# Unread whole-array products in the attention steps with heads of 8

## The chip, the cores and the metric

The kernel runs on one core of one Trainium2 chip. The metric is the device time of an execution in microseconds; lower is better. A core has a matrix engine (TensorE, in the profile PE for products and PEld for weight loads), a vector engine (VectorE, DVE), an activation engine (ScalarE, ACT), GpSimd (POOL) and DMA queues (SPq and others). [...]

## The reference

A batch of 16 sequences of 256 tokens with 128 channels goes through four layers. Each layer adds an attention (16 heads) and a feed-forward network. All four attentions look at the same context of 1601 rows of 64 channels; layers 0 and 2 also have an attention of the sequence to itself. In layers 0, 1 and 3 a head has 8 channels, in layer 2 it has 32. Cut to what matters:

```python
# layers 0, 1 and 3: x (16, 256, 128), ctx (16, 1601, 64), H = 16, D = 8
q = heads(norm(x) @ Wq); k = heads(ctx @ Wk); v = heads(ctx @ Wv)
a = softmax(einsum('bhqd,bhkd->bhqk', q, k) * D ** -0.5)
x = x + merge(einsum('bhqk,bhkd->bhqd', a, v)) @ Wo
x = x + ffn(norm(x))
# layer 2: the same with D = 32
```

## The kernel before, in words

**Two sequences at a time.** The kernel takes the sequences in eight rounds of two lanes. The list `seq` has, for every round, layer 0 of both, then layer 1 of both, then 2, then 3. Each entry is one attention over the context, and this main line of attentions is the frame of the whole program.

**Slabs and steps.** An attention is cut into four slabs of four heads (`Slab`). Four heads stand at partitions 0, 32, 64 and 96, so that a score product uses 32 rows of the array. With heads of 8 the 32 rows hold the high and low parts of queries and keys, which gives the float32 product from a shorter format. The 1601 keys are 13 tiles of 128 rows; a slab has seven steps of two tiles each, and the seventh has one tile of 65 keys.

**What a step does on TensorE, in program order.** The loop at the end of `model` writes the instructions in the order in which they are to run (`tc.manual_schedule()`), and TensorE takes its products in that order:

1. About half of the step's maxima of the *next* slab: a product of queries by 400 keys into a bank (`maxima`, from line 544), which VectorE reduces to a row maximum (line 552). A slab has 32 of them, five or six to a step.
2. The step's scores, transposed, into a double bank `st` (`st_ops`), with the maxima subtracted by bfloat16 products of ones by `nmT`. ScalarE turns them into probabilities (`exps`, line 464).
3. The rest of the step's maxima.
4. The weighing of the step before (`weigh_back`, which calls `weigh`): probabilities times values into the slab's accumulator bank `av`. With heads of 8, each of four heads has 9 columns (8 values and a sum) and only the first half of the bank, `av[:, 0, :]`, is used; with heads of 32 the second half takes the sums.
5. Two slots (`slot()`; three ahead of layer 2). A slot lets each of the side programs go on to its next `yield`: feed-forward networks, norms, the attention of a sequence to itself, keys and values of coming attentions (`key_line`, `value_line`).

All products are issued through the helper `mm` at line 172, so the profile gives them one line, and they are told apart by tiles: `bank<-k,q` are maxima, `st<-q,k` and `st<-nmT,ones` scores, `bank<-p,v` the weighing. A weighing product in float32 has two rows in the trace.

**Banks.** `bank()` deals out four banks. One is held by `av`, so the maxima wait for VectorE after three. The slots' products take theirs from the same four.

**The end of a slab.** After the last weighing, `finish` copies `av[:, 0, :]` out with ScalarE, transposes and divides. The maxima of the next slab are gathered (`thirds`, on VectorE and GpSimd) and transposed (`shift`, TensorE), which makes its `nmT`.

**Constants.** `ident16` is a 128x128 identity and `ones16` a 128x128 block of ones, both bfloat16, made once at the start. The causal mask of the self-attentions uses `ident16` against a mask `caus` in the same way, with 512 columns.

Of the kernel before, what the change touches and what calls it, by code (L numbers as in the profile page):

```python
# [20 lines left out]
P = 128  # L21
# [53 lines left out]
def model(ctx: ExitStack, tc: tile.TileContext, d, out):  # L75
# [34 lines left out]
    ident16 = const.tile([P, P], BF16, name="ident16")  # L110
    nc.vector.tensor_copy(ident16, ident)
    ones16 = const.tile([P, P], BF16, name="ones16")
# [58 lines left out]
    def mm(o, l, r, start=True, stop=True, free=False):  # L171
        nc.tensor.matmul(out=o, lhsT=l, rhs=r, start=start, stop=stop, skip_group_check=free)  # L172
# [289 lines left out]
    def exps(att, sc, n, r):  # L462
        e = probs()
        nc.scalar.activation(e[:r, :, :n, :], sc[:r, :, :n, :], AF.Exp, scale=att.scale)  # L464
        return e

    def zeroed(att):
        a = bank().rearrange("p (u q) -> p u q", u=2)
        n = 1 if att.d8 else 2
        mm(a[:, :n, :], zero16[:, :P], zero16.unsqueeze(1).broadcast_to([1, n, T]), True, False, True)  # L470
        return a

    def weigh(att, s, av, pr, t0, n, r, last, heads=range(4), sums=True, values=True):
        for i in range(n):
            fin = last and i == n - 1
            if values:
                for g in heads:
                    m = 9 if att.d8 else 32
                    mm(av[32 * g : 32 * g + m, 0, :], att.value(s, t0 + i, g, r), pr[g // 2][:r, g % 2, i, :],
                       False, fin, True)  # L480
            if sums and not att.d8:
                for g in heads:
                    mm(av[32 * g : 32 * g + 32, 1, :], ones[:r, :32], pr[g // 2][:r, g % 2, i, :], False, fin, True)

    def normalised(att, s, av):
        if att.d8:
            y = chan("y8")[:, :T]
            evac(y, av[:, 0, :])
            yield
            t = bank()  # L490
            for q in range(2):
                nc.tensor.transpose(t[:, q * P : (q + 1) * P], y[:, q * P : (q + 1) * P], ident)  # L492
            tv = t[:, :T].rearrange("p (q g e) -> p q g e", q=2, g=4)
            rc = sm.tile([P, 2, 4], F32, tag="rc8", name=name("rc8"))
            nc.vector.reciprocal(rc, tv[:, :, :, 8])
            nc.vector.tensor_tensor(
                att.o[:, :, 32 * s : 32 * s + 32].rearrange("p q (g e) -> p q g e", g=4),
                tv[:, :, :, :8], rc.unsqueeze(3).broadcast_to([P, 2, 4, 8]), ALU.mult,
            )
        else:  # L500
            rc = chan("rc")[:, :T]
            nc.vector.reciprocal(rc, av[:, 1, :])  # L502
            nc.vector.tensor_tensor(att.o[:, s, :], av[:, 0, :], rc, ALU.mult)
# [23 lines left out]
    class Slab:  # L527
# [16 lines left out]
        def maxima(self):  # L544

            g, q, c, k0, k1 = self.todo.popleft()
            att, s = self.att, self.s
            p = bank()
            h = slice(32 * g, 32 * g + 32)

            def reduce():
                nc.vector.tensor_reduce(self.mx[:, q, g, c : c + 1], p[:, : k1 - k0], AX.X, ALU.max)  # L552

            return lambda: mm(p[:, : k1 - k0], att.q[h, s, q * P : (q + 1) * P], att.k[s][h, k0:k1]), reduce
# [501 lines left out]
    def advance(g):  # L1056
        try:
            return True, next(g)
        except StopIteration:
            return False, None  # L1060

    def begin():

        while began[0] < nb:
            b = began[0]
            n = None if b < LANES else seq.index((b - LANES, "l3"))
            if n is not None and not (n in k_done and n in v_done):
                return
            chains.append([None, load_ctx(b)])
            chains.append([b, life(b)])  # L1070
            began[0] += 1

    def slot():
        begin()
        if later:
            g = later.popleft()
            if advance(g)[0]:
                later.appendleft(g)
        for i, l in enumerate(lines):
            if i == turn[0] % 2:  # L1080
                advance(l)
        turn[0] += 1
        for c in list(chains):
            if c[0] is not None and c[0] in ready:
                if not ready[c[0]].done:
                    continue
                del ready[c[0]]
            alive, att = advance(c[1])
            if att is not None:
                ready[c[0]] = att  # L1090
            if not alive:
                chains.remove(c)

    def until(cond):
        for _ in range(2000):
            if cond():
                return
            slot()
        raise RuntimeError("the slots do not come to an end")
# [3 lines left out]
    def slab(i):  # L1103

        n, s = divmod(i, 4)
        if n >= len(seq):
            return None
        b = seq[n][0]
        until(lambda: b in ready and not ready[b].done and n in k_of and s in k_of[n])
        att = ready[b]  # L1110
        att.k, att.v = k_of[n], v_of.setdefault(n, {})
        slabs_of[i] = Slab(att, s, i % 2)
        return slabs_of[i]

    def finish(sl, i):

        yield from normalised(sl.att, sl.s, sl.av)
        if sl.s == 3:
            sl.att.done = True
        if not sl.att.d8 or sl.s == 3:  # L1120
            vp_room.give()

    with tc.manual_schedule():
        sl = slab(0)
        while sl.todo:
            for o in sl.maxima():
                o()
        sl.thirds()
        sl.shift()
        back = None  # L1130

        def weigh_back():

            nonlocal back
            if back is None:
                return
            sl, i, j, pr = back
            n = i // 4
            t0, m, r = sl.steps[j]
            if j == 0:  # L1140
                until(lambda: (0 if sl.att.d8 else sl.s) in v_of.get(n, {}))
                sl.att.v = v_of[n]
                sl.av = zeroed(sl.att)
            last = j == len(sl.steps) - 1
            weigh(sl.att, sl.s, sl.av, pr, t0, m, r, last)
            back = None
            if last:
                g = finish(sl, i)
                if advance(g)[0]:
                    later.append(g)  # L1150

        for i in range(4 * len(seq)):
            nxt = slab(i + 1)
            steps = sl.steps
            emitted = 0

            def maxima(want):

                nonlocal emitted
                ops = []  # L1160
                while nxt is not None and emitted < want:
                    a, c = nxt.maxima()
                    a()
                    ops.append(c)
                    emitted += 1
                for c in ops:
                    c()

            for j, (t0, m, r) in enumerate(steps):

                part = 32 * (j + 1) // (len(steps) - 1)
                if j < len(steps) - 1:
                    maxima(part - 3)
                elif nxt is not None:
                    nxt.thirds()
                sc = st_ops(sl.att, sl.s, t0, m, r, sl.nmT)
                pr = [exps(sl.att, t, m, r) for t in sc]
                if j < len(steps) - 1:
                    maxima(part)
                weigh_back()  # L1180
                back = (sl, i, j, pr)
                if j == len(steps) - 1 and nxt is not None:
                    nxt.shift()
                slot()
                slot()

                if i // 4 + 1 < len(seq) and seq[i // 4 + 1][1] == "l2":
                    slot()
            kp_room.give()
            sl = nxt  # L1190
        weigh_back()
        until(lambda: not chains and not later)

# [118 lines left out]
```

## Time and profile before

| | |
|---|---|
| time, median of 3 | 11,063.08 us (11,060.85 to 11,069.93) |
| the profiled execution's time | 11,069.08 us |
| its span, first to last instruction | 11,067.1 us |
| mean granted TensorE clock | 0.815 |
| instructions | 204,917 |
| PE products, and their busy time | 86,834, 9,761.1 us |
| VectorE, ScalarE, GpSimd busy | 5,929.3, 4,978.5, 952.3 us |

The table is from the profile's page. Busy time is the time in which an engine has an instruction under way; products overlap in the array, so a busy PE is not PE at its peak. "Granted clock" is the share of TensorE's clock that the chip let through. An arrow in a row such as `bank<-p,v` reads "written from". The chain of waits is the series of instructions that ended last, followed back from the end, at each step to what released it.

### The profile page before, as it was taken

The numbers are of one execution on the slowest core, as the hardware profiler recorded it, in microseconds if no ns is written. First come the engines' busy times: TensorE is split into PE (matmuls) and PEld (weight loads), VectorE is DVE, ScalarE is ACT, GpSimd is POOL, SyncE is SP. The second block draws the span as 40 slices with busy tenths as digits, with TensorE's granted clock in tenths as the row PEclk, the third lists the DMA queues.
The fourth block names the chain that finished last, engine by engine and source line by source line (L and its number), as shares of the span: only waits on it lengthen the run. The fifth ranks groups of instructions, "written<-read, shape, count | busy, mean of one in ns | idle before, by whom it ended". The sixth has DMA issues, their size and how long they took to land.

```text
span 11067.1 us, 204917 instructions
## 1 busy us (share of the span) xinstructions
PE 9761.1 (88%) x86834; PEld 5294.4 (48%) x86874; DVE 5929.3 (54%) x13070; ACT 4978.5 (45%) x6812; POOL 952.3 (9%) x2283
## 2 busy tenths in 40 slices
PE   6989899897998979889798897998979889898898
PEld 3445444454444544445454454444545445444454
DVE  5545555455554555545455454554555545465455
ACT  3544455444553445434454344543445434454444
POOL 2000100001000010000100001000010000100000
PEclk8779777797878978789777897778977789687898
DMA  2100111001110011100111001110011100111011
GB/s 58 37 7 15 36 45 37 7 16 39 42 37 7 19 38 42 34 7 19 38 44 32 7 19 42 40 32 7 19 38 43 33 7 19 38 44 32 7 24 27
DMA packets 158828, 313.10 MB, mean 28 GB/s; under 512 B 65163, under 2 KB 116275, under 8 KB 157910
## 3 DMA queue, kind: packets, MB, share of 16 engines
q1 hardware_dynamic: 154676, 297.83, 11.7%
q8 instruction: 683, 11.19, 0.4%
q14 instruction: 235, 1.93, 0.1%
q0 software_dynamic: 768, 1.48, 0.0%
q10 hardware_dynamic: 2466, 0.68, 0.0%
HBM read 98.31 MB, written 2.10 MB: 9 GB/s over the span
## 4 chain that ended last, share of the span: by engine, by line
PE 71%; DVE 14%; ACT 5%; issue 4%; POOL 3%; SPq 2%; DMA 1%; another core or an unknown queue 0%; DVEq 0%; POOLq 0%; ACTq 0%
PE bank L172 57%; PE st L172 10%; DVE mx L552 5%; ACT p L464 3%; DVE nm L579 2%; SPq L411 2%; PE mx L172 1%; PE bank L492 1%; POOL p L603 1%; PE bank L298 1%; DVE z L282 1%; POOL rs L278 1%; DVE st L275 1%; DVE hl L405 1%; ACT y L239 1%
## 5 line engine op out<-in xcount | busy, mean ns | idle before, releaser
L552 DVE TENSOR_REDUCE mx<-bank 128x1 f32<-128x400 f32 (+2 forms) x8192 | 4155.2, 567 | 2296.9 <-PE bank L172 2271.8
L464 ACT ACTIVATE p<-st 128x1024 f32<-128x1024 f32 (+1 forms) x3840 | 3500.5, 963 | 3568.3 <-PE st L172 2358.6
L172 PE MATMUL bank<-k,q 32*128 32x400 f32 (+2 forms) x10240 | 3573.1, 557 | 495.3 <-DVE mx L552 261.3
L172 PEld LDWEIGHTS bank<-k,q 32*128 32x128 f32 x10240 | 1600.6, 211 | 1928.7 <-DVE mx L552 1111.4
L172 PE MATMUL bank<-p,v 128*9 128x256 f32 (+3 forms) x27648 | 2412.4, 460 | 12.6 <-POOL p L603 12.6
L172 PE MATMUL st<-q,k 32*128 32x256 f32 (+1 forms) x18176 | 1974.8, 391 | 126.2 <-DVE nm L579 69.2
L172 PEld LDWEIGHTS st<-q,k 32*128 32x128 f32 (+1 forms) x18176 | 1300.8, 210 | 443.7 <-ACT p L464 140.4
L172 PE MATMUL st<-nmT,ones 32*128 32x512 bf16 (+1 forms) x7680 | 1270.1, 435 | 0.0
L172 PEld LDWEIGHTS bank<-p,v 128*9 128x9 f32 (+3 forms) x27648 | 676.3, 104 | 1175.4 <-issue 922.6
L172 PE MATMUL bank<-p,ones 128*32 128x256 f32 (+1 forms) x7680 | 607.1, 389 | 18.1 <-ACT p L464 18.1
L509 POOL CAST nmp<-nm 128x8 bf16<-128x8 f32 x384 | 83.6, 218 | 5441.9 <-DVE nm L558 3668.7
L278 POOL TENSOR_TENSOR rs<-rs,neghalf 128x2 f32<-128x2 f32 x240 | 167.5, 698 | 3491.1 <-DVE rs L277 3491.1
L172 PEld LDWEIGHTS <-ones 32*128 32x128 bf16 (+1 forms) x7680 | 408.1, 108 | 39.4
L579 DVE TENSOR_REDUCE nm<-mx 128x4 f32<-128x1024 f32 x256 | 301.8, 1221 | 215.3 <-PE mx L172 210.6
L239 ACT COPY v<-bank 128x512 f32<-128x512 f32 (+3 forms) x592 | 228.6, 448 | 328.8 <-PE bank L172 328.8
L172 PEld LDWEIGHTS bank<-p,ones 128*32 128x32 f32 (+1 forms) x7680 | 250.8, 113 | 216.6 <-ACT p L464 43.6
L502 DVE RECIPROCAL rc<-bank 128x256 f32<-128x256 f32 x128 | 224.9, 1757 | 193.6 <-PE bank L172 189.3
L603 POOL TENSOR_SCALAR_AFFINE_SELECT p<-p 128x1024 f32<-128x1024 f32 x256 | 266.6, 1063 | 653.3 <-PE bank L172 352.7
L464 ACT ACT_TABLE_LOAD x141 | 180.9, 1283 | 312.9 <-PE st L172 201.9
L172 PE MATMUL bank<-ws,h 128*128 128x128 f32 x1664 | 297.9, 343 | 3.2 <-DVE h L1027 0.8
L768 DVE TENSOR_TENSOR x<-bank,x 128x256 f32<-128x256 f32 x144 | 61.1, 425 | 446.0 <-PE bank L172 446.0
L172 PEld LDWEIGHTS bank<-ws,h 128*128 128x128 f32 x1664 | 267.2, 248 | 39.0 <-DVE mx L552 13.6
(240 smaller groups left out, 7274.4 us busy)
## 6 DMA issues: line engine op xcount, KB each, us to landing
k<-hl SPq DMA_DIRECT2D x768, 200.2 KB, 4.0
q<-hl SPq DMA_DIRECT2D x1024, 32.0 KB, 1.9
ws<-in_s_l_a_li_dram SPq DMA_DIRECT2D x32, 768.0 KB, 4.3
ws<-in_s_l3f_dram SPq DMA_DIRECT2D x32, 768.0 KB, 6.7
ws<-in_s_l0f_dram SPq DMA_DIRECT2D x32, 512.0 KB, 5.6
ws<-in_s_l_a_qkv_dram SPq DMA_DIRECT2D x16, 768.0 KB
k<-hl SPq DMA_DIRECT2D x256, 32.0 KB, 1.9
ws<-in_s_l3f_dram SPq DMA_DIRECT2D x16, 384.0 KB
```

The lines of the kernel that those rows point to most:

```text
L172: nc.tensor.matmul(out=o, lhsT=l, rhs=r, start=start, stop=stop, skip_group_check=free)
L239: nc.scalar.copy(o, i)
L275: nc.vector.bn_stats(out=st[:, q, :], in_=src[:, q, :])
L278: nc.gpsimd.tensor_tensor(rs, rs, neghalf[:, 0:2], ALU.pow)
L282: nc.vector.tensor_scalar(z[:, q, :], src[:, q, :], mv[:, q, 0:1], rs[:, q : q + 1], ALU.subtract, ALU.mult)
L298: nc.tensor.transpose(p[:, q * P : (q + 1) * P], z[:, q, :], ident)
L411: nc.sync.dma_start(out=raw(o)[r::4, :], in_=raw(hl[c])[32 * s : 32 * s + 32, :])
L464: nc.scalar.activation(e[:r, :, :n, :], sc[:r, :, :n, :], AF.Exp, scale=att.scale)
L502: nc.vector.reciprocal(rc, av[:, 1, :])
L552: nc.vector.tensor_reduce(self.mx[:, q, g, c : c + 1], p[:, : k1 - k0], AX.X, ALU.max)
L579: nc.vector.tensor_reduce(o, sc[hp], AX.X, ALU.max, negate=True)
L603: nc.gpsimd.affine_select(out=e, in_=e, pattern=[[0, 2], [sign * P, 2], [-sign, T]], compare_op=op, fill=0.0, base=0, channel_multiplier=sign,
```

## The change

A new helper writes `n` products of `ident16` (weights, the whole array) by `ones16` repeated to 256 columns, in bfloat16, into the second half of the accumulator bank of the slab at hand. With heads of 8 nobody reads that half. Three of them follow each weighing but the slab's last, and three more are written after the slots of that step; the flag `open_av` says that a weighing was the last thing put into an unfinished bank. Nothing else moves. The blank lines are as in the kernel.

```diff
+    def keep_up(av, n):
+
+
+        for _ in range(n):
+            mm(av[:, 1, :], ident16, ones16.unsqueeze(1).broadcast_to([P, 2, P]), False, False, True)

     def normalised(att, s, av):
...
         back = None
+        open_av = [None]
...
             weigh(sl.att, sl.s, sl.av, pr, t0, m, r, last)
             back = None
+            if sl.att.d8 and not last:
+                keep_up(sl.av, 3)
+                open_av[0] = sl.av
+            else:
+                open_av[0] = None
             if last:
...
                 if i // 4 + 1 < len(seq) and seq[i // 4 + 1][1] == "l2":
                     slot()
+                if open_av[0] is not None:
+                    keep_up(open_av[0], 3)
             kp_room.give()
```

There are 48 attentions with heads of 8, so 192 slabs and 1152 weighings that are followed by products.

## The prediction

> **What bounds the kernel now.** I read the page's engine and clock rows first, then windows of 3 us, the timeline of some steps, the chain of waits, and last a tally of my own over the trace.
>
> On the page, TensorE is the only engine near full, and its granted clock lies at 0.7 to 0.8 over most of the span:
>
> ```profile
> PE 9761.1 (88%) x86834; PEld 5294.4 (48%) x86874; DVE 5929.3 (54%) x13070; ACT 4978.5 (45%) x6812; POOL 952.3 (9%) x2283
> ...
> PEclk8779777797878978789777897778977789687898
> ```
>
> The windows resolve that mean. Columns: stretch, length, busy us of PE, PEld, DVE, ACT, POOL, the clock, DMA:
>
> ```profile
> 1604.00:1607.00 3.00, 3.00 (x30) 1.27 (x29) 1.20 (x4) 1.02 (x2) 0.00 (x0) 0.50 0.00 0
> 1613.00:1616.00 3.00, 2.93 (x34) 1.49 (x26) 2.55 (x6) 2.22 (x4) 0.00 (x0) 1.00 0.00 0
> ```
>
> The clock is full or half, nothing between, and a PE without a gap can be at half. The timeline shows the price:
>
> ```profile
> 1599.57 1.90 PE L172 MATMUL bank<-p,v 128*9 128x256 f32 x16
> ...
> 1604.35 1.90 PE L172 MATMUL bank<-p,v 128*9 128x256 f32 x16
> ...
> 1612.69 1.05 PE L172 MATMUL bank<-p,v 128*9 128x256 f32 x16
> ...
> 1613.67 0.53 PE L172 MATMUL bank<-k,q 32*128 32x400 f32 x3
> ...
> 1614.16 2.98 DVE L552 TENSOR_REDUCE mx<-bank 128x1 f32<-128x400 f32 x6 [0.45 <-PE bank L172]
> ...
> 1614.79 1.40 PE L172 MATMUL bank<-k,q 32*128 32x400 f32 x3
> ...
> 1616.12 1.05 PE L172 MATMUL bank<-p,v 128*9 128x256 f32 x16
> ```
>
> The 16 rows of `bank<-p,v` are one step's weighing. From one to the next a step with six maxima takes 4.78 us at half clock (1599.57 to 1604.35) and 3.43 at full (1612.69 to 1616.12). At full clock VectorE works 2.98 of the 3.43 and idles only the 0.45 until the first new score bank comes. PE runs weighing, three maxima, scores, then three maxima at VectorE's pace; these add up, none lies beside another. The chain of waits passes through PE in those same steps:
>
> ```profile
> 1602.98 3.79 PE bank L172 x20
> 1606.76 0.99 PE st L172 x8
> 1607.76 3.30 PE bank L172 x19
> ```
>
> The end of the weighing, where the products go, is on the chain in 932 of the 1143 places I could match (82%).
>
> Cut at each slab's last, short key tile (65 keys), the trace has 191 slabs with heads of 8: 7730 us, of which 3746 (48%) at half clock. The 64 slabs with heads of 32 take 3109 us, 8% of it at half. Equal slabs of the six middle rounds met the clock differently; comparing each only with its equals, a microsecond at half clock costs 0.287 us extra (standard error 0.007). So the most that a full clock could return in heads of 8 is 0.287 x 3746 = 1075 us: 6655 instead of 7730.
>
> **What the clock follows.** I tallied, per 3.41 us stretch, streamed columns times share of the array used (32 rows or 32 columns are a quarter), float32 rows twice, since 256 columns of them take as long as 512 of bfloat16 (216 ns). Share of stretches after which the clock was full:
>
> | tally | full before | half before |
> |---|---|---|
> | under 3000 | 4% of 191 | 1% of 492 |
> | 3000 to 3500 | 17% of 153 | 29% of 277 |
> | 3500 to 4000 | 63% of 131 | 66% of 285 |
> | 4000 to 4500 | 81% of 228 | 90% of 132 |
> | over 4500 | 100% of 1326 | 100% of 11 |
>
> So a stretch must hold some 3600 columns of whole-array work, in either state.
>
> [...] here a group of weighing rows follows the last after about 200 ns, but a 32-row product only after 309: about 0.1 us (0.15 at half clock).
>
> **The change, part by part.** Nothing is removed or moved on ACT, DVE, POOL or the DMA queues. PE gains 192 slabs x 6 of 7 steps = 1152 steps x 6 = 6912 products of 128x128 by 256 columns, each with its weight load, so 13,824 rows.
>
> *One product.* The nearest row is the causal mask, of the same operand kinds with 512 columns (shortest, median and longest ns of one by tile; then two pieces of the timeline):
>
> ```profile
> L172 PE MATMUL mx<-caus,ident x216: 379/607/634, 63.1 to 9632.9; 128*128 128x512 bf16 x108
> ```
>
> ```profile
> 1352.27 0.81 PE L172 MATMUL mx<-caus,ident 128*128 128x512 bf16 x3 [0.16 <-issue]
> ...
> 1363.04 1.48 PE L172 MATMUL mx<-caus,ident 128*128 128x512 bf16 x3 [0.33 <-issue]
> ```
>
> Three take 0.81 us of which the last is 0.379: 0.216 each at full clock, and (1.48 - 0.634)/2 = 0.42 at half. Half the columns: 0.108 and 0.213. Their weight loads lie behind the product before; uncovered, they would cost up to 0.1 each, the upper bound.
>
> *One step.* [...] 0.65 + 0.095 = 0.74 us at full clock, 1.28 + 0.15 = 1.43 at half. [...]
>
> *What it delays.* Behind the products in PE's queue are the slots' products and then the next maxima, for which VectorE waits: its idle 0.45 becomes 1.19, the full-clock step 4.17, the half-clock one about 6.2. Nothing covers that. Where the chain lies elsewhere (18% of the places; the next product is itself late by 0.03 to 0.04 us on average), part is absorbed. I take 12%, with 0 and 50% as ends. At full clock throughout: 1152 x 0.74 x 0.88 = 750 us.
>
> *What it does to the clock.* Six products add 1536 to a step's tally. A full-clock six-maxima step has 4784 in 3.43 us, already over 3600 in 3.41. A half-clock one has 4784 in 4.78, so 3416; with the products (4784 + 1536) in 6.2, so 3480: no denser, since at half clock they stream at the rate at which the weighing fills the array. The full clock is lost in stretches full of slot work and waits, and there few steps fall: 0.21 a stretch where the tally is under 3600, against 0.55 on average, so about 320 columns each. Putting the additions into every stretch of the trace, with its lengthening, and reading the chances again, the half-clock share falls from 48% to between 29 and 41%, as a product's columns count a quarter more or a fifth less than the fit's middle value. I take 36%.
>
> *Sum.* 6655 + 750 = 7405 us at full clock. At half clock a microsecond then does 0.31 less (0.287 before; the products themselves double). 7405 / (1 - 0.31 x 0.36) = 8336, which is 606 over 7730. The profiled execution took 11,069.1 us (span 11,067.1), 6 above the median 11,063.1; 11,069 + 606 - 6 = **11,670**. With 29% it is 11,470, with 41% 11,820.
>
> **Rivals.** *The clock does not move* (48%): 7405 / (1 - 0.31 x 0.48) = 8700, so 12,030; with nothing absorbed, 12,150. For it: the products add nothing to the density of a half-clock step, and constants might count for less. Against it: the causal mask, also against an identity, counts in a fit of the clock as a float32 row of twice its rate does.
>
> *The clock is held, and the kernel is faster.* The whole-array work before the slots' waits carries PE over the threshold, and the 1075 us come back against 750 spent: 7405 in heads of 8, so 10,740; with half absorbed, 10,410. It decides from where 7405 / (1 - 0.31x) falls under 7730, a half-clock share of 14%. For it: slabs with heads of 32, with denser steps, lie at 8%. Against it: the stretches that lose the clock hold few steps.
>
> *It doesn't cost what it seems:* the products fall into PE's idle time and move nothing. The order of instructions has all 6912 of them, in order after each weighing, on the chain; so this is small.
>
> **How the numbers follow.** A measurement of this kernel can tell about 0.2% (22 us). Forecast (partial gain, net loss) 0.69, clock unmoved 0.14, clock held 0.14, no net effect 0.03. That makes slower 0.83, same 0.03, faster 0.14. The range 11,050 to 12,150 takes in the forecast with its bounds and the unmoved clock, and leaves out the held clock and the uncovered weight loads.
>
> **What would show it.** In the changed profile: 6912 rows of `bank<-ones,ident` starting 0.108 or 0.213 apart; full-clock steps with six maxima at 4.17 us and VectorE's wait in them at 1.2; half-clock ones at 6.2; mean clock 0.86 (0.36 x 8336 = 3000 us at half in heads of 8 and the 339 elsewhere, of 11,670). A mean clock of 0.81 would mean the second case, one over 0.93 the third. Full-clock steps still at 3.43 would make the cost wrong; half-clock shares under 14% the clock part.

## The result, and the profile after

The changed kernel takes 11,395.6 us (median of 4 runs, 11,385 to 11,409). Against the kernel before, run beside it, the ratio is 1.0274 (95% interval 1.0251 to 1.0298): 2.7% slower, where 5.5% was forecast. In the experiments the kernel before took between 11,067 and 11,136 us, so what follows is given as ratios to its runs on the same chip.

The page of the profile after, with the engine row, the granted clock and the chain of waits by engine:

```profile
span 11400.1 us, 218787 instructions
...
PE 10158.3 (89%) x93786; PEld 5604.5 (49%) x93786; DVE 5925.4 (52%) x13070; ACT 4976.9 (44%) x6812; POOL 952.0 (8%) x2283
...
PEclk8889888898888978889788897888988889898898
...
PE 73%; DVE 14%; ACT 5%; issue 4%; POOL 3%; SPq 2%; DMA 1%; POOLq 0%; DVEq 0%; ACTq 0%
```

VectorE, ScalarE and GpSimd have the work they had; TensorE has about 400 us more of busy time, and most sevens of the clock row became eights: a mean of 0.878 against 0.815. More of the chain lies on PE, 73% against 71%. So the clock did rise, and the kernel is slower all the same. The new rows of the costliest groups:

```profile
L172 PE MATMUL bank<-ones,ident 128*128 128x256 bf16 x6912 | 1222.0, 304 | 0.0
...
L172 PEld LDWEIGHTS <-ident 128*128 128x128 bf16 x7168 | 623.0, 105 | 914.8 <-issue 807.2
```

The 304 ns are the mean length of one record; products overlap, so six of them follow each other faster (0.109 us from start to start at full clock, 0.213 at half, medians of 3960 and 1059 pairs). Columns: start, length, engine, line, what, and the idle time before with its releaser.

```profile
1688.31 1.05 PE L172 MATMUL bank<-p,v 128*9 128x256 f32 x16
...
1689.30 0.83 PE L172 MATMUL bank<-ones,ident 128*128 128x256 bf16 x6
...
1690.54 2.98 DVE L558 TENSOR_REDUCE mx<-bank 128x1 f32<-128x400 f32 x6 [1.21 <-PE bank L172]
...
1691.16 1.41 PE L172 MATMUL bank<-k,q 32*128 32x400 f32 x3 [0.19 <-DVE mx L558]
...
1692.50 1.05 PE L172 MATMUL bank<-p,v 128*9 128x256 f32 x16
```

This is a step with six maxima at full clock, 4.19 us from weighing to weighing; before it was 3.43. VectorE now stands idle for 1.21 us until the first maxima come, where it stood 0.45. At half clock such a step takes 6.17 us against 4.78.

**One account for the runs.** Each trace was cut into slabs as in the prediction. The 191 slabs with heads of 8 give a time and the part of it at half clock; comparing equal slabs of the six middle rounds gives, in each run, what a microsecond at half clock costs extra. Taking that off leaves what the slabs would take at full clock. Its rise over the 6655 us of before is the *price* of the products; the fall of the half-clock cost under the 1075 us of before is what the clock *returned*.

| kernel | ratio to before | clock | heads of 8, us | at half clock | extra per us | price | returned |
|---|---|---|---|---|---|---|---|
| before | 1 | 0.815 | 7730 | 3746 | 0.287 | | |
| changed | 1.0274 | 0.878 | 8035 | 2404 | 0.309 | 636 | 332 |
| changed, random data (e2) | 1.0263 | 0.879 | 8032 | 2391 | 0.336 | 573 | 272 |
| on 32 rows (e1) | 1.0823 | 0.769 | 8754 | 5284 | 0.323 | 392 | -632 |
| only behind the weighing (e7) | 1.0274 | 0.839 | 8063 | 3349 | 0.304 | 391 | 58 |
| only after the slots (e10) | 1.0068 | 0.855 | 7817 | 2920 | 0.294 | 304 | 218 |
| ahead of the transposes (e3) | 0.9910 | 0.837 | 7637 | 3204 | 0.297 | 30 | 123 |
| three between the maxima (e4) | 0.9850 | 0.851 | 7654 | 2958 | 0.296 | 124 | 200 |
| six between the maxima (e5) | 0.9887 | 0.889 | 7624 | 2180 | 0.354 | 197 | 303 |
| e3 and e4 together (e6) | 0.9782 | 0.874 | 7501 | 2393 | 0.311 | 101 | 330 |
| e6 with four between the maxima (e8) | 0.9787 | 0.879 | 7529 | 2268 | 0.303 | 186 | 388 |
| e8 with four before the shift (e9) | 0.9814 | 0.883 | 7505 | 2156 | 0.314 | 173 | 399 |

The changed kernel's 636 less 332 is 304 of the 333 us by which its span grew. The rest lies in the 64 slabs with heads of 32 (3109 to 3136 us; 300 us at half clock where it was 249) and at the ends.

The account is good to some 60 us. The standard errors of "extra per us" are 0.005 to 0.015, which makes 20 to 50 us in a price or a return, and e2, the same program with other operands, differs from the changed kernel by 63 and 60. Each row also comes from one profiled execution: that of e4 took 10,977 us at a clock of 0.851, its other three 10,925 to 10,938 at 0.857 to 0.860, so its row makes e4 look worse than its ratio does. There is a second way to a price that doesn't use the clock's cost: the mean rise of each of a slab's seven steps over the kernel before, only where both were at full clock, summed over 192 slabs. It gives 702 us for the changed kernel, 384 for e7, 351 for e10, 8 for e3, 71 for e4, 253 for e5 and 74 for e6. The places come out in the same order, but for e4 and e6, which are alike.

### The profile page after: what moved, and what is told of

Read it like the earlier page. It is cut to its first block, busy times and chain, and to the rows that moved or that the text cites. A ratio compares the mean times of both kernels' runs of the same rounds, so it can differ in the third digit from the quotient of the medians.

```text
span 11400.1 us, 218787 instructions
## 1 busy us (share of the span) xinstructions
PE 10158.3 (89%) x93786; PEld 5604.5 (49%) x93786; DVE 5925.4 (52%) x13070; ACT 4976.9 (44%) x6812; POOL 952.0 (8%) x2283
## 4 chain that ended last, share of the span: by engine, by line
PE 73%; DVE 14%; ACT 5%; issue 4%; POOL 3%; SPq 2%; DMA 1%; POOLq 0%; DVEq 0%; ACTq 0%
PE bank L172 61%; PE st L172 8%; DVE mx L558 5%; ACT p L464 2%; DVE nm L585 2%; SPq L411 2%; PE mx L172 1%; PE bank L498 1%; POOL p L609 1%; DVE z L282 1%; POOL rs L278 1%; DVE st L275 1%; PE bank L298 1%; DVE hl L405 1%; DVE mv L276 1%
## 5 line engine op out<-in xcount | busy, mean ns | idle before, releaser
L172 PE MATMUL bank<-k,q 32*128 32x400 f32 (+2 forms) x10240 | 3344.8, 523 | 497.7 <-DVE mx L558 330.9
L172 PEld LDWEIGHTS bank<-k,q 32*128 32x128 f32 x10240 | 1467.7, 198 | 1731.4 <-DVE mx L558 1097.5
L172 PE MATMUL bank<-p,v 128*9 128x256 f32 (+3 forms) x27648 | 2240.2, 431 | 12.6 <-POOL p L609 12.6
L172 PE MATMUL st<-q,k 32*128 32x256 f32 (+1 forms) x18176 | 1837.3, 370 | 91.8 <-DVE nm L585 49.2
L172 PEld LDWEIGHTS st<-q,k 32*128 32x128 f32 (+1 forms) x18176 | 1204.1, 196 | 328.0 <-issue 98.2
L172 PE MATMUL bank<-ones,ident 128*128 128x256 bf16 x6912 | 1222.0, 304 | 0.0
L172 PE MATMUL st<-nmT,ones 32*128 32x512 bf16 (+1 forms) x7680 | 1167.9, 395 | 0.0
L172 PEld LDWEIGHTS <-ident 128*128 128x128 bf16 x7168 | 623.0, 105 | 914.8 <-issue 807.2
L172 PEld LDWEIGHTS <-ones 32*128 32x128 bf16 (+1 forms) x7680 | 380.1, 100 | 31.2
```

## The experiments

The theory: the products stand where VectorE has run dry and cost their stream there; the clock follows how much of the array is used, and returns only part. The rivals: any work on TensorE would raise the clock; the data matter; the price is the gap of about 0.1 us on either side of the products, or their number, not their place.

### e1_quarter: the same products on 32 rows

```diff
-            mm(av[:, 1, :], ident16, ones16.unsqueeze(1).broadcast_to([P, 2, P]), False, False, True)
+            mm(av[:, 1, :], ident16[:32, :], ones16[:32, :].unsqueeze(1).broadcast_to([32, 2, P]), False, False, True)
```

> The changed kernel with its 6912 products made on 32 rows of the array instead of 128 (the same 256 columns streamed, a quarter of the whole-array tally). Theory A, the clock follows the share of the array that is used: the price stays near 0.65 us in a full-clock step (from one weighing to the next with six maxima 4.1 us), but the clock gain goes: mean clock 0.81 to 0.84, time 11,600 to 11,850. Rival B, any product that keeps TensorE going raises the clock: clock 0.87 to 0.88 as in the changed kernel, time 11,300 to 11,420.

Measured: 12,017 us, ratio 1.0823 (1.0802 to 1.0843), clock 0.769. The page's engine and clock rows of this run:

```profile
PE 10941.8 (91%) x93786; PEld 6019.7 (50%) x93786; DVE 5932.8 (49%) x13070; ACT 4987.0 (41%) x6812; POOL 951.1 (8%) x2283
...
PEclk7689676896768967689667896668966689766896
```

TensorE is busier than in any other run, 91%, and has the lowest clock. The rival that any work raises the clock falls. The direction of the theory holds, but both sizes were off, and the time lies above the expected 11,850. A full-clock step with six maxima took 3.84 us instead of the expected 4.1, and the clock did not stay: it fell under that of before. In terms of the tally, a thin product (one on few rows) takes time without filling the array, so it dilutes the stretch it stands in; half-clock stretches were followed by full clock in 22% of cases, against 34% before and 48% in the changed kernel. The step grew by only 0.41 us because thin products run beside the maxima, as in this piece of the timeline at full clock:

```profile
1648.19 0.28 PE L172 MATMUL bank<-ones,ident 32*128 32x256 bf16 x1
1648.20 0.47 PE L172 MATMUL bank<-k,q 32*128 32x400 f32 x1
1648.31 0.46 PE L172 MATMUL bank<-ones,ident 32*128 32x256 bf16 x2
```

A maximum starts 0.01 us after a thin product; behind a whole-array one it starts 0.20 us later.

### e2_random: random data in the same products

```diff
-            mm(av[:, 1, :], ident16, ones16.unsqueeze(1).broadcast_to([P, 2, P]), False, False, True)
+            mm(av[:, 1, :], rnd16, rnd16.unsqueeze(1).broadcast_to([P, 2, P]), False, False, True)
```

> The changed kernel with a random bfloat16 matrix (a copy of one layer's query weights) as both operands of the products, instead of identity and ones. Theory A, the clock follows which part of the array is used and for how long, not the data: clock 0.87 to 0.885, time within 0.4% of the changed kernel, 11,350 to 11,440. Rival B, toggling data counts and constants count for less: clock 0.90 or more and the time under 11,300.

Measured: 11,395 us, ratio 1.0263 (1.0237 to 1.0288), clock 0.879 against 0.878. Identity and ones serve as well as this random matrix; the rival falls.

### e3_y6: products in the wait ahead of the transposes

The steps are those of the kernel before; the products stand in `normalised`.

```diff
             t = bank()
+            for _ in range(6):
+                mm(t[:, T:], ident16, ones16.unsqueeze(1).broadcast_to([P, 2, P]), True, True, True)
             for q in range(2):
                 nc.tensor.transpose(t[:, q * P : (q + 1) * P], y[:, q * P : (q + 1) * P], ident)
```

> The kernel before with no products in the steps, and six whole-array products in the unused half of the bank into which each slab's result is transposed, ahead of those transposes, where TensorE waits for ScalarE's copy of y in the trace of before (205 waits, 0.7 us each). Theory A, products in a wait cost nothing and the thin stretch at a slab's end gets its columns: half-clock share with heads of 8 from 48% to 38-44%, clock 0.82 to 0.85, time 10,900 to 11,040. Rival B, the wait is not there any more at that place or the stretches that lose the clock lie elsewhere: clock 0.81 to 0.82, time 11,060 to 11,200.

Measured: 11,000 us, ratio 0.9910 (0.9890 to 0.9930), clock 0.837. What released TensorE's products and weight loads on the tile `y` after idle time (us in total, times), first in the kernel before, then here:

```profile
  ACT y L239: 405.4, 409
```

```profile
  ACT y L239: 43.3, 143
```

The wait is filled, and the price of 1536 products is 30 us, which the account can't tell from nothing. Of the stretches after which the full clock was lost, 97 held such a transpose before, and 5 do here. Theory A holds. But most of these losses came back in other places: in all, the full clock was lost 381 times, against 404 before.

### e4_mid3 and e5_mid6: products ahead of the second maxima

The products behind the weighing and after the slots are taken out; `open_av` stays. The number is 3 in e4 and 6 in e5.

```diff
                 if j < len(steps) - 1:
+                    if open_av[0] is not None:
+                        keep_up(open_av[0], 3)
                     maxima(part)
```

> Three products instead of six, moved: none after the weighing or the slots, but three between the score products and the second half of the maxima, in five of seven steps of a slab (2880 products). Theory A, there TensorE would wait for VectorE to free banks, so a full-clock step with six maxima goes from 3.43 to at most 3.6 us, half-clock ones to 5.3; clock 0.83 to 0.86, time 11,000 to 11,150. Rival B, [...] full-clock step 3.9 to 4.0, time 11,200 to 11,350.

Measured for e4: 10,932 us, ratio 0.9850 (0.9832 to 0.9867), clock 0.851. The timeline of a full-clock step with six maxima:

```profile
1600.01 1.05 PE L172 MATMUL bank<-p,v 128*9 128x256 f32 x16
...
1601.48 3.08 DVE L558 TENSOR_REDUCE mx<-bank 128x1 f32<-128x400 f32 x6 [0.27 <-PE bank L172]
...
1602.11 0.50 PE L172 MATMUL bank<-ones,ident 128*128 128x256 bf16 x3
...
1602.54 0.97 PE L172 MATMUL bank<-k,q 32*128 32x400 f32 x3
1603.44 1.05 PE L172 MATMUL bank<-p,v 128*9 128x256 f32 x16
```

3.43 us from weighing to weighing, with three products in it: in this step they cost nothing. VectorE still has banks to reduce when they start, and the second maxima, late by the products, come before it is done. Matched step by step with the kernel before, at full clock in both, the mean difference is 0.01 us over 143 steps without slot products and 0.04 over 106 with them. The half-clock steps with six maxima and products took 4.78, as before. The exception is the set between a slab's sixth weighing and its last: there the mean difference is 0.26 us over 106 steps. Only two maxima stand ahead of the products in that step, and VectorE runs dry (in the one that starts at 1614.12 us it waits 0.24 us for the third). So the wait is what makes the place cheap. Rival B, the same price in any place, had this step at 3.9 to 4.0 us. Theory A holds, and the time came out 68 us under its range.

> Six products a step as in the changed kernel, but all between the scores and the second half of the maxima, where three cost nothing in a full-clock step (3.43 us with and without them). 5760 products in five of seven steps. Theory A, the price of the changed kernel comes from the place behind the weighing, where VectorE has run dry: a full-clock step with six maxima takes 3.45 to 3.8 us instead of 4.19, clock 0.86 to 0.88, time 10,850 to 11,080. Rival B, three were cheap because they were few, and six cost their stream: full-clock step 4.1 or more, time over 11,250.

Measured for e5: 10,947 us, ratio 0.9887 (0.9846 to 0.9928), clock 0.889, the highest of the profiled executions. A full-clock step takes 3.67 us where the same six products in the changed kernel make it 4.19, so most of the price came from the place and not from the number. But here the cover is used up:

```profile
1599.58 0.83 PE L172 MATMUL bank<-ones,ident 128*128 128x256 bf16 x6
...
1600.82 1.06 DVE L558 TENSOR_REDUCE mx<-bank 128x1 f32<-128x400 f32 x2 [0.70 <-PE bank L172]
```

VectorE waits 0.70 us instead of 0.27 to 0.45. By the account the higher clock returns 103 us more than with three, and the price takes 73 of it; the measured ratios, 0.9887 and 0.9850, show no gain over three, and their intervals overlap.

### e6_y6mid3: both cheap places

> Both cheap places together: six products ahead of the transposes of y and three between scores and second maxima. Theory A, they feed different thin stretches and add: 0.9% and 1.5% give 2.0 to 2.5% under the kernel before, clock 0.86 to 0.88, half-clock share with heads of 8 under 33%. Rival B, they cure the same stretches: 1.4 to 1.8%, clock 0.85.

Measured: 10,846 us, ratio 0.9782 (0.9757 to 0.9807), clock 0.874; half-clock share with heads of 8 2393 of 7501 us, 32%. The page's rows:

```profile
PE 9708.9 (90%) x91287; PEld 5296.6 (49%) x91287; DVE 5976.1 (55%) x13070; ACT 4983.8 (46%) x6812; POOL 955.9 (9%) x2283
...
PEclk8889888898888979889898897988978889788898
```

It is 2.2% under the kernel before, where 0.9% and 1.5% would add up to 2.4: theory A, within the interval. This version beats both kernels: nearly the changed kernel's clock for a price of 101 us instead of 636. TensorE's busy time is even less than the 9761 us of the kernel before.

### e7_first3 and e10_slots3: half the dose, in either place

e7 leaves out the three products after the slots, e10 the three behind the weighing.

```diff
-                if open_av[0] is not None:
-                    keep_up(open_av[0], 3)
```

```diff
-                keep_up(sl.av, 3)
```

> The changed kernel with only the three products behind each weighing (3456), none after the slots. Theory A, price and gain go with the number: full-clock step with six maxima 3.43 + 0.33 + 0.1 = 3.85 us, half of the 636 us of price, half or more of the clock gain, ratio to before 1.005 to 1.018, clock 0.845 to 0.865. Rival B, [...] full-clock step over 4.0, ratio over 1.02. Rival C, the clock needs the whole dose: clock under 0.83.

Measured for e7: 11,389 us, ratio 1.0274 (1.0252 to 1.0296), clock 0.839. The step is as theory A has it (3.86 us), but its ratio and clock miss the range: half the products take 391 of the 636 us of price and return 58 of the 332. Rival B, by which most of the price is the gap of about 0.1 us on either side of the products, has its ratio (over 1.02) but not its step (over 4.0), so its cause isn't the one, and rival C's clock (under 0.83) didn't come either.

> The changed kernel with only the three products after the slots (3456), none behind the weighing: the other half of the dose. Where a step has no slot products, this is the same program as with only the first three. Theory A, the clock answers more than in proportion to the dose, wherever the half dose stands: clock 0.83 to 0.85, ratio 1.018 to 1.032, full-clock step 3.86. Rival B, the place after the slots is what holds the clock: clock 0.86 or more, ratio under 1.012.

Measured for e10: 11,164 us, ratio 1.0068 (1.0034 to 1.0102), clock 0.855 (0.840 to 0.857 over its seven executions, of 11,129 to 11,249 us). The step is again 3.86 us, but the return is 218 us, against 58. That speaks for rival B, the place after the slots, though the clock stays a little under its range. The dose alone is not what counts: the two halves together give prices of 695 and returns of 276, near the 636 and 332 of the whole, but the shares of the return are unlike. In steps with slot products the place after the slots is also cheaper (0.21 us a step against 0.28, matched at full clock). Why it returns so much more isn't settled. The clock's record shows one difference: the full clock was lost 468 times in e7 and 359 times in e10, against 404 before, while a half-clock stretch was followed by full clock in 44% and 38%. By these counts the products after the slots help to keep the clock, and those behind the weighing don't. A likely reason is that the weighing before the first place is already dense, while slot work and maxima around the second are thin; no run shows it by itself.

### e8_y6mid4 and e9_y6mid4sh4: more in the cheap places

e8 puts four products instead of three ahead of the second maxima of e6; e9 adds four to `shift_T`:

```diff
             m = min(2, len(ns) - s0)
+            for _ in range(4 if len(ns) == 1 else 0):
+                mm(p[:, T:], ident16, ones16.unsqueeze(1).broadcast_to([P, 2, P]), True, True, True)
```

> As the combined version, but four instead of three products between scores and second maxima. Theory A, the wait for VectorE there hides about 0.6 us (three cost nothing, six cost 0.24), so four cost at most 0.05 us a full-clock step and bring some clock: ratio to before 0.972 to 0.979, clock 0.875 to 0.89. Rival B, the cover is used up at three: full-clock step 3.5 or more, ratio 0.98 or more.

> The run before it, and four products in the free half of the bank of each slab's `shift`, ahead of its products, which wait for GpSimd (184 waits, some 180 us, in the combined version). Theory A, they stand in a wait: ratio 0.966 to 0.976, below the run without them, clock up by 0.005 or more. Rival B, most shifts don't wait, and 256 x 4 products cost up to 110 us: ratio 0.98 or more.

Measured: e8 0.9787 (0.9759 to 0.9814) at clock 0.879; e9 0.9814 (0.9786 to 0.9842) at 0.883. In e8 the fourth product is as free in full-clock steps without slot products (3.43 us) as A has it. The clock rose a little in both, and the time didn't fall against e6's 0.9782; e8's ratio lies at the end of A's range, e9's in B's. The intervals overlap, so that e9 is worse is not shown. By the account both return more than e6 (388 and 399 against 330) and pay more for it (186 and 173 against 101): these places had little left to give.

## Why the prediction was right, and where it was off

**The bound and the place: right.** The products stand on the chain, VectorE waits for what is queued behind them, and nothing covers that in a step without slot products. Six products: 0.74 us predicted at full clock (0.65 for six in a row, 0.095 for one more gap like that between a weighing and a maximum), 0.76 measured (4.19 less 3.43); 1.43 and 1.39 at half. VectorE's wait: 1.19 and 1.21. The causal mask was the right row to take the price from, and the weight loads are hidden: at full clock the new products start 0.109 us apart, and the causal mask's, of twice the columns, 0.216, with a load of 0.098 us (median) for each product of either kind. e4 and e5 show that the place makes the price. One reading was wrong without harm to the sum: that of a step's parts "none lies beside another". In the timeline shown there, three maxima and the scores start 0.10 us apart (1613.67 and 1613.77) and overlap.

**What is absorbed: too little.** I took 12%, so a price of 750 us; the account gives 636 of the 852, 25%. It could be anything from 18% (702 us, the matched steps) to 33% (573 us, e2). Matched step by step at full clock, 217 steps without slot products rose by 0.76 us in the middle, 152 with slot products by only 0.57 (mean 0.53). There two terms of the sum were too high. Where a slot product on the whole array comes next, no further gap is added: it starts 0.11 us after the last of the new products, where a maximum starts 0.20 us after it. And part of the rest, by my estimate, fell into waits; no run shows that by itself. By the account this took 114 us off.

**The half-clock share: the term that was mis-sized most.** I took 36%; it is 30% (2404 of 8035). At 0.309 a microsecond (0.31 was predicted) that is a half-clock cost of 744 us instead of 931, so 187 us less. The step that failed is "no denser": it compared a half-clock step's mean tally, 3480 for 3.41 us, with the 3600 that I had read from the tally. A stretch, 3.41 us, is only about half as long as such a step, 6.17 us, and a weighing with six products behind it (1.8 and 1.3 us at half clock) nearly fills one. In half-clock stretches wholly within steps without slot products, the median tally went from 3517 (137 stretches) to 3901 (73), and the chance that full clock follows from 26 to 80%. Half-clock steps of this kind with six maxima fell from 45 to 10. So in these steps one dense stretch could raise the clock where the mean of the step would not. The 36% itself was read from the additions to every stretch, with a product's columns at the middle value of a fit; at the end where they count a quarter more, 29%, it was about right. Which part of the miss is the weight and which the spreading within a step isn't separated.

Price and clock together are the 301 us by which 8336 was above the measured 8035; both were off to the same side, so neither hid the other. The forecast took the other slabs as unchanged; they grew by 27 us or so.

**The rivals.** An unmoved clock is refuted by 0.878. e1 shows what does move it: the part of the array that is used, as the tally had it (the same number of products and columns, 0.769 on 32 rows and 0.878 on 128). The held clock, with its point at a share of 14%, did not come: it is still lost nearly as often, 397 times against 404; what changed most is how soon it comes back (half-clock stretches followed by full clock: 34 to 48%). As there are more stretches at full clock, the share of them after which it is lost fell too, from 20 to 16%. Against 332 us returned stand 636 paid. Even a clock at full throughout would have returned 1075, leaving 439 us; the gain was there to be had, but at another place.

## What to carry to other kernels

Before you add filler to lift TensorE's clock, price it by its place. Behind the weighing, with VectorE idle until the next maxima, six products cost their whole stream here (0.76 us of a full-clock step); ahead of the second maxima, in a wait for VectorE, three cost 0.01 to 0.04 us, and six, which outlast the wait, 0.24 (3.67 less 3.43). The chain of waits and the idle time of the next engine tell which place it is. Count what it adds as columns times the part of the array used, since work on a quarter of the array lowered the clock here that it was meant to raise (0.769, from 0.815). And judge the clock by the densest stretch as well as by the mean: in steps without slot products, half-clock stretches were followed by full clock in 26% of cases before and in 80% with the products.

## What the runs showed of the hardware

- In the clock's record of the kernel before, the granted clock is full or half and nothing between, and each of the 807 pieces at one clock (without the one cut off at the end) lasts a whole number of times 3.413 us, from 1 to 32; so does each of the 793 in the changed kernel.
- The clock went with how much of the array was used in a stretch, not with how busy TensorE was: 91% busy at a clock of 0.769 in e1, 88% at 0.815 before, 89% at 0.878 in the changed kernel. Before, 678 stretches of 3.41 us at half clock had TensorE busy throughout, and 317 of them were followed by half clock again. Two kinds of operand data made no difference (0.879 and 0.878). The tally sorts the stretches well; that 32 rows count just a quarter was assumed in it, and no run here measures that weight. That a float32 row counts twice rests on its time: at full clock, whole-array products of 256 float32 columns start 0.216 us apart, as those of 512 bfloat16 columns do.
- The tally's 3600, an estimate from the stretches of before, carried over: in the changed kernel stretches of 3500 to 4000 were followed by full clock in 51% (from full) and 76% (from half), over 4500 in 1745 of 1748, under 3000 in none of 433.
- Six products on 32 rows lengthened a full-clock step by 0.41 us, less than the 0.65 of their own columns: they run partly beside the 32-row maxima and scores next to them (a maximum starts 0.01 us after one in e1, 0.20 us after a whole-array product in the changed kernel).
- Between the weighing's products and those on the whole array, or between these and 32-row ones, about 0.1 us is added at full clock and 0.15 at half. From the last row of a weighing to the first new product it is 0.31 us (0.56 at half), where weighing groups follow each other after 0.20 (0.41). From the last new product to a maximum it is 0.20 (0.35), where two of the new products start 0.11 apart (0.21).
